# Root of the feed-forward norm moved from GpSimd to VectorE, and new ranks for the instruction order of a two-layer recurrent block

## The chip, the cores and the metric

The kernel is one program on one core of a Trainium2 chip. The metric is device time in microseconds, the median over runs of one launch; lower is better. Times inside the program come from one profiled execution.

## What is computed

Two layers over x of shape (4, 512, 128): batch B = 4, T = 512 tokens, D = 128. Each layer is `x = x + attention(xn) * silu(experts(xn))`, with `xn` the layer norm of `x`.

```python
x = L0_attn_x
xn = _layernorm(x, axis=-1)
s = _L0_attn_ref(xn, ...)              # 16 heads of 8; keys of the last 64 tokens; weighted scores
g = _silu(_L0_ffn_ref(xn, ...))        # 8 experts 128-512-128, gelu, one chosen per token
x = x + s * g
xn = _layernorm(x, axis=-1)
s = _L1_attn_ref(xn, ...)              # norm, windowed attention, projection, residual, and:
#   h = layernorm(out, ln2_g, ln2_b)
#   h = gelu(h @ w1 + b1);  h = h @ w2 + b2;  return h + residual2
g = _silu(_L1_ffn_ref(xn, ...))        # 8 experts 128-512-128, relu, one chosen per token
x = x + s * g
```

The first half of the change is in the `layernorm(out, ln2_g, ln2_b)` of layer 1's own feed forward: the term `1 / sqrt(v + EPS)` for each token.

## The kernel before, in words

**Tiles.** Tokens lie on the 128 partitions. A batch is NT = 4 tiles of 128 tokens; 16 tiles in all. For the experts the tokens of all batches are sorted by expert into NBLK = 23 blocks of 128 rows for each layer.

**Threads.** The work is written as 32 Python generators ("threads"), each a chain of steps over its batches, tiles or blocks. Layer 0: `prepare0` (norm, gate), `route` (sorts tokens to blocks), `moe_load` and `moe_load_2` (a gather of a block's tokens, issued by GpSimd, and its weights), `moe_x`, `moe_h`, `moe_y` (transpose, first and second matrix of a block; `moe_y` ends in a scatter of the block, issued by GpSimd, L666), `gates`, `project0`, `scores_q`, `fitness0`, `masked0` (q spread over heads by GpSimd, L1069), `scores_k`, `values0`, `outs0`, `combine0`. Layer 1: `prepare1` (norm, its root by GpSimd at L442), the same expert threads, `project1`, `queries1` (its q4 is made by GpSimd, L1251), `scores_k1`, `values1`, `outs1`, `contexts1`, `feed1`, `combine1`.

**Order.** Each engine runs its instructions in the order in which it was given them. That order is settled at build time by `run`: a greedy planner that holds a time `now["T"]` for TensorE and a list of taken slots for VectorE ("D"), ScalarE ("A"), GpSimd ("G") and SyncE's queue ("Q"). At each turn it takes, among the threads' next steps, the one that can start first, and among those that can start now the one with the lowest rank. A thread has four ranks, one for each batch (for the expert threads, for each quarter of the blocks). Each step gives its costs by `spent(cost, steps)`: `cost` is TensorE's time, stretched by `pace()`, and `steps` are the pieces of work on the other engines, put into the first free slot. `settle` then makes the order of the slots the order of the instructions on VectorE, ScalarE and GpSimd. So the ranks, the paces and the costs touch no arithmetic, but together they decide the place of nearly every instruction. Where the planner sees TensorE idle, `awake` adds multiplications with ones (bf16, 128x512), whose result is overwritten, to keep it busy.

**The norm of the feed forward.** `feed1` runs eight times, for each batch and each pair of tiles (u = 0, 2). A turn: projection `pr` into PSUM; residual added by VectorE (L1431); moments (L416, L417); the root; `centred` (L428) writes hn; TensorE transposes it (`tr_hn`); ScalarE copies it as hT; then two matrices with gelu between (`f`, `fy`) and the last add (L1468). The root before is `rsqrt`: VectorE adds EPS (L392), GpSimd raises to the power -0.5 (L393), and VectorE's `centred` waits for it:

```python
nc.vector.tensor_scalar_add(dst, src, eps)                                                    # L392
return nc.gpsimd.tensor_tensor(dst, dst, neghalf[:, 0:1].to_broadcast([P, n]), ALU.pow)       # L393
```

`rsqrt_many`, which `project0` already uses for 128 columns, does the same by VectorE alone: four instructions for x and a first guess from the bits, then three Newton steps of three instructions.

GpSimd's line thus holds, in layer 1: roots of `prepare1` (L442), gathers `xb` (L609), scatters `yt` (L666), `q` (L1251), adds `xr` (L1402, L1437) and the roots `rs_d` (L393).

Of the kernel before, what the change touches and what calls it, by code (L numbers as in the profile page):

```python
# [9 lines left out]
F32 = mybir.dt.float32  # L10
# [6 lines left out]
P = 128  # L17
B, T, D = 4, 512, 128
NT = T // P
H, HD = 16, 8  # L20
G, J = 4, 4
# [15 lines left out]
LN_EPS = 1e-5  # L37
# [20 lines left out]
def two_layers(  # L58
# [212 lines left out]
    def after(event):  # L271

        return None, max(0.0, at[event] - max(now["T"], now["-"]))
# [51 lines left out]
            at[e] = t  # L325

    def pace():
        return 1.8 if now["T"] < 70.0 else 1.12

    def behind_steps(e, t):  # L330

# [57 lines left out]
    def rsqrt(dst, src, eps):  # L389

        n = dst.shape[1]
        nc.vector.tensor_scalar_add(dst, src, eps)  # L392
        return nc.gpsimd.tensor_tensor(dst, dst, neghalf[:, 0:1].to_broadcast([P, n]), ALU.pow)  # L393

    def rsqrt_many(dst, src, scale, eps):

        n = dst.shape[1]
        x = small.tile([P, n], F32, tag="rq_x", name=f"rq_x_{dst.tensor.name}", bufs=1)
        nc.vector.tensor_scalar(x, src, scale, eps, ALU.mult, ALU.add)
        y = small.tile([P, n], F32, tag="rq_y", name=f"rq_y_{dst.tensor.name}", bufs=1)  # L400
        nc.vector.tensor_single_scalar(y.bitcast(I32), x.bitcast(I32), 1, ALU.logical_shift_right)
        nc.vector.tensor_scalar(y.bitcast(I32), y.bitcast(I32), -1.0, float(0x5F3759DF), ALU.mult, ALU.add)
        nc.vector.tensor_scalar_mul(x, x, -0.5)
        z = small.tile([P, n], F32, tag="rq_z", name=f"rq_z_{dst.tensor.name}", bufs=1)
        for i in range(3):
            nc.vector.tensor_tensor(z, y, y, ALU.mult)
            nc.vector.tensor_tensor(z, z, x, ALU.mult)
            nc.vector.scalar_tensor_tensor(dst if i == 2 else y, z, 1.5, y, ALU.add, ALU.mult)
# [83 lines left out]
    def route(mask, n):  # L492
# [7 lines left out]
        with tc.high_priority():  # L500
            ps = bank(f"rk_{n}")
            mm(ps[:, 0 : NTOK * E], before_m, mask.rearrange("p i e -> p (i e)"), start=True, stop=True)
            mm(ps[:, NTOK * E : 2 * NTOK * E], ones, mask.rearrange("p i e -> p (i e)"), start=True, stop=True)
            cnt = of([P, E, NTOK], "cnt")
            nc.vector.tensor_copy(cnt, ps[:, NTOK * E : 2 * NTOK * E].rearrange("p (i e) -> p e i", e=E))
            inc = of([P, E, NTOK], "inc")
            nc.vector.tensor_tensor_scan(
                inc.rearrange("p e i -> p (e i)"), go_on.rearrange("p e i -> p (e i)"),
                cnt.rearrange("p e i -> p (e i)"), 0.0, ALU.mult, ALU.add,
            )  # L510
            some = of([P, E, NTOK], "some")
            nc.vector.tensor_tensor(
                some, inc[:, :, NTOK - 1 : NTOK].to_broadcast([P, E, NTOK]),
                tile_at[:, None, :].to_broadcast([P, E, NTOK]), ALU.is_gt,
            )
            nb = of([P, E], "nb")
            nc.vector.tensor_reduce(nb, some, AX.X, ALU.add)
            ends = of([P, E], "ends")
            nc.vector.tensor_tensor_scan(ends, ones[:, 0:E], nb, 0.0, ALU.mult, ALU.add)

            nc.vector.tensor_tensor(inc, inc, cnt, ALU.subtract)
            starts = of([P, E], "starts")
            nc.vector.tensor_tensor(starts, ends, nb, ALU.subtract)
            nc.vector.scalar_tensor_tensor(
                inc, starts[:, :, None].to_broadcast([P, E, NTOK]), float(P), inc, ALU.mult, ALU.add
            )
            at = small.tile([P, NTOK, E], F32, tag="rt_some", name=f"at_{n}", bufs=1)
            nc.vector.tensor_tensor(
                at, ps[:, 0 : NTOK * E].rearrange("p (i e) -> p i e", e=E), inc.rearrange("p e i -> p i e"), ALU.add
            )  # L530
            nc.vector.tensor_tensor(at, at, mask, ALU.mult)
            rowf = of([P, NTOK], "rowf")
            nc.vector.tensor_reduce(rowf, at, AX.X, ALU.add)
            rows_at = of([P, NTOK], "rows_at", I32)
            nc.vector.tensor_copy(rows_at, rowf)

            blk = of([P, NTOK], "blk", I32)
            nc.vector.tensor_single_scalar(blk, rows_at, 7, ALU.logical_shift_right)
            blkf = of([P, NTOK], "blkf")
            nc.vector.tensor_copy(blkf, blk)  # L540
            placef = of([P, NTOK], "placef")
            nc.vector.scalar_tensor_tensor(placef, blkf, -float(P), rowf, ALU.mult, ALU.add)

            tok_blk = of([P, NTOK, 3, NBLK], "tok_blk", BF16)
            in_blk = tok_blk[:, :, 2]
            nc.vector.tensor_tensor(
                in_blk, blkf[:, :, None].to_broadcast([P, NTOK, NBLK]),
                block_at[:, None, :].to_broadcast([P, NTOK, NBLK]), ALU.is_equal,
            )
            nc.vector.tensor_tensor(  # L550
                tok_blk[:, :, 0], in_blk, tile_at[:, :, None].to_broadcast([P, NTOK, NBLK]), ALU.mult
            )
            nc.vector.tensor_scalar_mul(tok_blk[:, :, 1], in_blk, pidx)
            spent(0.35, [("D", 1.0)] * 7, [("rows", n)])
            in_places = []
            for q in range(2):
                in_place = att_p.tile([P, NTOK // 2, P], BF16, tag="osb0", name=f"in_place_{n}_{q}")
                i = q * NTOK // 2
                for u in range(NTOK // 2):
                    nc.vector.tensor_single_scalar(in_place[:, u], place_at, placef[:, i + u : i + u + 1], ALU.is_equal)  # L560
                in_places.append(in_place)
                spent(0, [after(("rows", n)), ("D", 1.2)], [("places", n, q)])

            past = of([1, NBLK, E], "past")
            nc.vector.tensor_tensor(
                past, ends[0:1, None, :].to_broadcast([1, NBLK, E]),
                block_at[0:1, :, None].to_broadcast([1, NBLK, E]), ALU.is_le,
            )
            ofx = of([1, NBLK], "ofx")
            nc.vector.tensor_reduce(ofx, past, AX.X, ALU.add)  # L570
            which = of([1, NBLK], "which", I32)
            nc.vector.tensor_single_scalar(which, ofx, float(E - 1), ALU.min)
            spent(0, [after(("rows", n)), ("D", 0.8)], [("which", n)])
# [839 lines left out]
    def feed1():  # L1413


        for b in range(B):
            for u in range(0, NT, 2):
                two = slice(u, u + 2)
                f = slice(u * P, (u + 2) * P)
# [11 lines left out]
                nc.vector.tensor_tensor(res[:, two], ps, res[:, two], ALU.add)  # L1431
                mv = moments(res[:, two], f"d{b}_{u}")
                rs = small.tile([P, 2], F32, tag="rs", name=f"rs_d{b}_{u}")
                rsqrt(rs, mv[:, :, 1], LN_EPS)
                centred(hn[:, two], res[:, two], mv, rs)
                spent(1.0, [("D", 0.7), ("D", 0.7), ("G", 1.0), ("D", 0.7)], [("pr", b, u)])
                nc.gpsimd.tensor_tensor(  # L1437
                    res[:, two], res[:, two], row("ffn2")[:, None, :].to_broadcast([P, 2, D]), ALU.add
                )
# [31 lines left out]
    def combine1():  # L1471
# [10 lines left out]
    KQ, Q4 = 1, 2  # L1482
    at["x"] = 0.0
    run([
        (moe_h(0, gelu), 0, 59, 111, 16),
        (scores_k1(), 87, 25, 32, 64),
        (project1(), 92, 81, 14, 102),
        (queries1(), 107, 26, 4, 78),
        (combine0(), 19, 20, 21, 22),
        (moe_load(0, xd0, w1_0, C_B1_0), 109, 42, 85, 68),  # L1490
        (moe_load_2(0, w2_0, b2_0), 18, 74, 23, 2),
        (gates(0, yt0), 56, 5, 6, 8),
        (values1(), 66, 112, 86, 55),
        (prepare0(), 31, 65, 95, 50),
        (moe_load(1, xd1, w1_1, C_B1_1), 35, 84, 34, 38),
        (moe_load_2(1, w2_1, b2_1), 101, 118, 37, 44),
        (scores_q(), 70, 36, 104, 94),
        (moe_x(0), 73, 93, 43, 96),
        (contexts1(), 11, 12, 54, 13),
        (project0(), 88, 106, 63, 62),  # L1500
        (moe_y(0, yt0), 117, 82, 90, 41),
        (moe_x(1), 67, 40, 46, 72),
        (gates(1, yt1), 103, 49, 114, 10),
        (values0(), 48, 15, 115, 124),
        (scores_k(), 33, 1, 58, 97),
        (route(mask0, 0), 45, 100, 24, 76),
        (fitness0(), 79, 61, 91, 69),
        (combine1(), 29, 30, 39, 99),
        (route(mask1, 1), 51, 83, 9, 75),
        (moe_y(1, yt1), 121, 71, 113, 127),  # L1510
        (outs0(), 47, 57, 125, 119),
        (masked0(), 7, 52, 53, 17),
        (moe_h(1, relu), 60, 3, 122, 105),
        (prepare1(), 27, 108, 28, 80),
        (outs1(), 120, 110, 116, 89),
        (feed1(), 126, 98, 123, 77),
    ])


# [42 lines left out]
```

## Time and profile before

| what | us |
|---|---|
| median of 3 runs | 510.99 (509.62 to 512.5) |
| time of the profiled execution | 499.03 |
| its span, first to last instruction | 497.3 |
| TensorE busy (multiplications) | 417.26 |
| VectorE busy | 337.45 |
| ScalarE busy | 261.61 |
| GpSimd busy | 179.69 |

The mean granted TensorE clock is 0.918. The span is the sum of what lies between the first and the last instruction; 1.7 us lie around it. In the profile's timeline a row is a start, a length, the engine, the line of the kernel, the operation, output <- input, the shape and the count; in brackets stands the time the engine was idle before and what released it. Table rows for a stretch give busy time and, in brackets, the number of instructions for each engine, then the granted clock, the busy share of the DMA engines and GB/s. A tile's buffer number is left out of its name.

### The profile page before, as it was taken

To read this page: it belongs to the slowest core of one execution; us is meant where nothing else is said; L and a number is where in the kernel's file an instruction comes from. 1 tells how busy PE (TensorE), PEld (TensorE's weight loads), DVE (VectorE), ACT (ScalarE), POOL (GpSimd) and SP (SyncE) were. 2 spreads that over 40 slices of the span, in tenths; PEclk is the share of its full clock that TensorE was granted. 3 is DMA by queue.
4 is the path that set the end of the run, shared out by engine and by line. 5 is a ranking of instruction groups with operands and counts; after the bars stand their busy time and mean duration, and the time that the engine had idled before them with its cause. 6 is when DMAs were issued, how large, how long until landed. Compare 5 with 4: busy or idle time off the path is not lost.

```text
span 497.3 us, 14720 instructions
## 1 busy us (share of the span) xinstructions
PE 417.3 (84%) x5663; PEld 295.0 (59%) x5663; DVE 337.5 (68%) x1013; ACT 261.6 (53%) x513; POOL 179.7 (36%) x251
## 2 busy tenths in 40 slices
PE   5876897998899696599999896878999994699985
PEld 2642565676565462345655574646879883588863
DVE  6899997553846958958774584884677761475565
ACT  1422665697567534375555655444676442246622
POOL 5741455346522222233320304136352335642311
PEclk8787699999999967779999998998999998599999
DMA  5405454756243010100000000051453773352032
GB/s 170 130 1 135 111 156 114 211 152 202 50 109 96 12 54 22 43 22 3 3 22 3 3 1 22 2 150 30 130 140 102 176 200 100 109 134 77 19 105 66
DMA packets 61894, 42.12 MB, mean 85 GB/s; under 512 B 11328, under 2 KB 54208, under 8 KB 61824
## 3 DMA queue, kind: packets, MB, share of 16 engines
q1 hardware_dynamic: 58464, 34.85, 25.3%
q0 software_dynamic: 2944, 6.04, 4.5%
q8 instruction: 45, 0.74, 0.6%
q10 hardware_dynamic: 416, 0.29, 0.3%
q14 instruction: 25, 0.20, 0.1%
HBM read 34.99 MB, written 6.16 MB: 83 GB/s over the span
## 4 chain that ended last, share of the span: by engine, by line
PE 47%; DVE 27%; issue 9%; ACT 7%; POOL 5%; DMA 3%; SPq 0%; POOLq 0%; ACTq 0%; DVEq 0%
PE e L83 8%; PE h L83 6%; PE s L83 5%; PE y L83 4%; PE ov L83 4%; DVE mx L1009 3%; DVE mx L1290 3%; PE fy L83 3%; PE f L83 2%; ACT th L1017 2%; PE o L88 2%; ACT pt L1106 2%; PE qkv L83 1%; PE v L83 1%; DVE sm L1009 1%
## 5 line engine op out<-in xcount | busy, mean ns | idle before, releaser
L666 POOL DMA_INDIRECT yt<-yb,put_at x46 | 46.1, 1002 | 104.3 <-DVE yb L664 24.8
L609 POOL DMA_INDIRECT xb<-xd,tokens_at x46 | 46.2, 1004 | 53.9 <-DVE tokens_at L586 17.1
L83 PE MATMUL y<-wb,hb 128*128 128x128 f32 x368 | 49.7, 285 | 4.3 <-ACT hb L696 3.2
L83 PE MATMUL h<-xbT,wb 128*128 128x128 f32 x368 | 51.2, 291 | 2.3 <-ACT xbT L344 1.3
L83 PEld LDWEIGHTS h<-xbT,wb 128*128 128x128 f32 x368 | 46.5, 202 | 8.5 <-issue 3.3
L83 PEld LDWEIGHTS y<-wb,hb 128*128 128x128 f32 x368 | 46.1, 198 | 7.7 <-ACT hb L696 3.9
L83 PE MATMUL e<-q,kd 32*64 32x256 f32 (+1 forms) x864 | 44.9, 457 | 0.4 <-ACT pt L1106 0.4
L1017 ACT ACTIVATE th<-s 128x768 f32<-128x768 f32 x32 | 26.0, 813 | 29.8 <-DVE mx L1009 29.2
L1333 ACT ACTIVATE pt<-e 128x1024 f32<-128x1024 f32 x32 | 31.0, 1021 | 19.9 <-PE e L83 19.8
L1290 DVE TENSOR_REDUCE mx<-s 128x16 f32<-128x1024 f32 x32 | 37.6, 1218 | 4.4 <-PE s L83 4.2
L83 PE MATMUL s<-k,qd 32*32 32x384 f32 (+1 forms) x1024 | 37.2, 484 | 2.6 <-ACT pt L1333 2.3
L1106 ACT ACTIVATE pt<-e 128x1024 f32<-128x1024 f32 x32 | 31.0, 1021 | 14.2 <-PE e L83 14.1
L83 PEld LDWEIGHTS <-ones 12*64 12x64 bf16 (+2 forms) x439 | 21.5, 107 | 28.6 <-issue 20.4
L1009 DVE TENSOR_REDUCE mx<-s 128x8 f32<-128x768 f32 x32 | 29.3, 949 | 11.9 <-PE s L83 11.9
L344 ACT COPY osb<-ov 128x512 f32<-128x512 f32 x33 | 18.6, 587 | 26.8 <-PE ov L83 21.4
L696 ACT ACTIVATE hb<-h,bb 128x128 f32<-128x128 f32 x92 | 26.5, 382 | 11.3 <-PE h L83 10.2
L1009 DVE TENSOR_REDUCE sm<-th 128x8 f32<-128x768 f32 x32 | 30.0, 946 | 1.3 <-ACT th L1017 1.0
L83 PE MATMUL ov<-pt,va 64*32 64x128 f32 (+1 forms) x896 | 28.8, 290 | 0.4 <-DVE ctx L344 0.2
L83 PEld LDWEIGHTS e<-q,kd 32*64 32x64 f32 x864 | 19.4, 139 | 11.5 <-issue 6.4
L1251 POOL TENSOR_TENSOR q<-qd,jmask 128x640 f32<-128x640 f32 x16 | 20.0, 1260 | 14.7 <-PE e L83 13.4
L83 PE MATMUL e<-sh,ones 12*64 12x256 bf16 (+1 forms) x320 | 20.8, 311 | 3.6 <-DVE sh L1301 3.6
L704 ACT ACTIVATE hb<-h,bb 128x128 f32<-128x128 f32 x56 | 15.8, 376 | 14.7 <-PE h L83 12.0
(287 smaller groups left out, 898.1 us busy)
## 6 DMA issues: line engine op xcount, KB each, us to landing
wb<-in_w SPq DMA_DIRECT2D x92, 256.0 KB
bb<-in_b SPq DMA_DIRECT2D x46, 64.0 KB
acc<-yt SPq DMA_DIRECT2D x8, 256.0 KB
xd<-ln_a SPq DMA_DIRECT2D x4, 256.0 KB
xd<-xr SPq DMA_DIRECT2D x4, 256.0 KB
out<-acc SPq DMA_DIRECT2D x8, 128.0 KB
x<-in_x SPq DMA_DIRECT2D x3, 256.0 KB
bb<-in_cols SPq DMA_DIRECT2D x46, 2.0 KB
```

Of the source, the lines that this page charges most:

```text
L83: ins = nc.tensor.matmul(*args, **kw)
L344: (nc.scalar.copy if e == "A" else nc.vector.tensor_copy)(dst, src)
L609: nc.gpsimd.indirect_dma_start(out=xb, out_offset=None, in_=xd, in_offset=bass.IndirectOffsetOnAxis(ap=tokens_at[:, k : k + 1], axis=0),)
L666: nc.gpsimd.indirect_dma_start(out=yt, out_offset=bass.IndirectOffsetOnAxis(ap=routed[n][0][:, k : k + 1], axis=0), in_=y, in_offset=None,)
L696: nc.scalar.activation(h[:, c, :], src[:, c * P : (c + 1) * P], AF.Gelu, bias=bias[:, c : c + 1])
L704: nc.scalar.activation(dst, src_c, AF.Relu, bias=b)
L1009: nc.vector.tensor_reduce(dst[:, t, 8 * gg : 8 * gg + 8].rearrange("p (u j) -> p u j", u=2), src.rearrange("p u (j f) -> p u j f", j=J), A ...
L1017: nc.scalar.activation(th, ps[gg], AF.Tanh, scale=0.5 * SCALE)
L1106: nc.scalar.activation(pt[:, 2 * gg : 2 * gg + 2], ps[gg], AF.Exp)
L1251: engine.tensor_tensor(dst, src[:, None, o : o + TW].to_broadcast([P, J, TW]), jmask[:, :, None].to_broadcast([P, J, TW]), ALU.mult,)
L1290: nc.vector.tensor_reduce(mx.rearrange("p a g j -> p g a j")[:, 2 * gg : 2 * gg + 2], ps[gg], AX.X, ALU.max, negate=True,)
L1333: nc.scalar.activation(pt[:, 2 * gg : 2 * gg + 2], ps[gg], AF.Exp, scale=SCALE)
```

## The change

Three edits. The root in `feed1` is taken by `rsqrt_many` (13 VectorE instructions on 2 columns, among them the add of EPS) in place of `rsqrt`; its temporary tiles get a common width of 128 columns, of which the first n are used. The planner's costs are altered: the pace of TensorE, the VectorE costs of `route`, and the steps of the norm (four on VectorE in place of two on VectorE, one on GpSimd and one on VectorE). And all 128 ranks are new.

```diff
     def pace():
-        return 1.8 if now["T"] < 70.0 else 1.12
+        return 1.45 if now["T"] < 70.0 else 1.08
...
     def rsqrt_many(dst, src, scale, eps):

         n = dst.shape[1]
-        x = small.tile([P, n], F32, tag="rq_x", name=f"rq_x_{dst.tensor.name}", bufs=1)
+        x = small.tile([P, P], F32, tag="rq_x", name=f"rq_x_{dst.tensor.name}", bufs=1)[:, 0:n]
         nc.vector.tensor_scalar(x, src, scale, eps, ALU.mult, ALU.add)
...
-            spent(0.35, [("D", 1.0)] * 7, [("rows", n)])
+            spent(0.35, [("D", 0.47)] * 7, [("rows", n)])
...
-                spent(0, [after(("rows", n)), ("D", 1.2)], [("places", n, q)])
+                spent(0, [after(("rows", n)), ("D", 0.65)], [("places", n, q)])
...
                 rs = small.tile([P, 2], F32, tag="rs", name=f"rs_d{b}_{u}")
-                rsqrt(rs, mv[:, :, 1], LN_EPS)
+                rsqrt_many(rs, mv[:, :, 1], 1.0, LN_EPS)
                 centred(hn[:, two], res[:, two], mv, rs)
-                spent(1.0, [("D", 0.7), ("D", 0.7), ("G", 1.0), ("D", 0.7)], [("pr", b, u)])
+                spent(1.0, [("D", 0.7), ("D", 0.75), ("D", 0.75), ("D", 0.75)], [("pr", b, u)])
...
     run([
-        (moe_h(0, gelu), 0, 59, 111, 16),
-        (scores_k1(), 87, 25, 32, 64),
-        (project1(), 92, 81, 14, 102),
-        (queries1(), 107, 26, 4, 78),
+        (moe_h(0, gelu), 32, 76, 48, 83),
+        (scores_k1(), 38, 74, 77, 63),
+        (project1(), 115, 64, 19, 52),
+        (queries1(), 61, 28, 17, 69),
...
-        (values1(), 66, 112, 86, 55),
+        (values1(), 86, 20, 30, 112),
...
-        (contexts1(), 11, 12, 54, 13),
+        (contexts1(), 102, 15, 107, 119),
...
-        (moe_y(1, yt1), 121, 71, 113, 127),
+        (moe_y(1, yt1), 85, 11, 114, 53),
...
-        (moe_h(1, relu), 60, 3, 122, 105),
+        (moe_h(1, relu), 120, 99, 66, 95),
...
-        (outs1(), 120, 110, 116, 89),
-        (feed1(), 126, 98, 123, 77),
+        (outs1(), 1, 45, 121, 82),
+        (feed1(), 109, 7, 14, 55),
     ])
```

The called function, with the lines of before:

```python
x = ...                                                                       # [P, n]
nc.vector.tensor_scalar(x, src, scale, eps, ALU.mult, ALU.add)                # L399
nc.vector.tensor_single_scalar(y.bitcast(I32), x.bitcast(I32), 1, ALU.logical_shift_right)
nc.vector.tensor_scalar(y.bitcast(I32), y.bitcast(I32), -1.0, float(0x5F3759DF), ALU.mult, ALU.add)
nc.vector.tensor_scalar_mul(x, x, -0.5)
for i in range(3):
    nc.vector.tensor_tensor(z, y, y, ALU.mult)                                # L406
    nc.vector.tensor_tensor(z, z, x, ALU.mult)
    nc.vector.scalar_tensor_tensor(dst if i == 2 else y, z, 1.5, y, ALU.add, ALU.mult)
```

## The prediction

> **What bounds the kernel now.** I read the page first: the busy row, the slices, the chain by engine.
>
> ```profile
> PE 417.3 (84%) x5663; PEld 295.0 (59%) x5663; DVE 337.5 (68%) x1013; ACT 261.6 (53%) x513; POOL 179.7 (36%) x251
> PE   5876897998899696599999896878999994699985
> PE 47%; DVE 27%; issue 9%; ACT 7%; POOL 5%; DMA 3%; SPq 0%; POOLq 0%; ACTq 0%; DVEq 0%
> ```
>
> TensorE (PE) is the fullest line and nearly half of the chain. VectorE (DVE) carries a quarter, GpSimd (POOL) a twentieth. In the slices (12.4 us each) the digits 4 and 6 after the long run of nines are the hole to look at. The table by stretches measures it:
>
> ```profile
> 345.00:412.00 67.00, 63.89 (x1045) 54.65 (x1045) 45.27 (x133) 39.36 (x94) 25.81 (x29) 1.00 0.55 146
> 412.00:428.00 16.00, 4.24 (x55) 3.25 (x54) 1.43 (x6) 2.29 (x9) 10.67 (x11) 0.72 0.25 67
> 428.00:470.00 42.00, 41.55 (x672) 35.16 (x670) 26.96 (x89) 23.83 (x48) 16.69 (x20) 0.94 0.35 93
> ```
>
> Columns: TensorE, its weight loads, VectorE, ScalarE, GpSimd, then clock, DMA share, GB/s. Before and behind the hole TensorE is full, so time won in it is kept to about 470. In it only GpSimd works. The waits name who held whom, in total us, times, longest:
>
> ```profile
> DVE hn L428 <- POOL rs_d L393: 21.9, 8, 14.6
> PE tr_hn L88 <- DVE hn L428: 13.8, 3, 11.8
> POOL yt L666 <- DMA yt<-yb,put_at: 11.3, 5, 4.2
> ```
>
> So hn waits for the root 21.9 us over eight turns, one wait being 14.6, and TensorE loses 11.8 of that. GpSimd's timeline says why:
>
> ```profile
> 412.49 0.96 POOL L666 DMA_INDIRECT yt<-yb,put_at  x1 [2.09 <-DVE sh L1301]
> 413.76 0.98 POOL L609 DMA_INDIRECT xb<-xd,tokens_at  x1 [0.30 <-PE s L83]
> 417.44 0.96 POOL L666 DMA_INDIRECT yt<-yb,put_at  x1 [2.70 <-ACT hb L704]
> 418.41 2.48 POOL L1251 TENSOR_TENSOR q<-qd,jmask 128x640 f32<-128x640 f32 x2
> 421.06 1.00 POOL L666 DMA_INDIRECT yt<-yb,put_at  x1 [0.17 <-issue]
> ...
> 424.90 1.00 POOL L666 DMA_INDIRECT yt<-yb,put_at  x1 [0.30 <-issue]
> 425.92 0.74 POOL L393 TENSOR_TENSOR rs_d<-rs_d,neghalf 128x2 f32<-128x2 f32 x1
> ```
>
> The root's input was ready at 411.1 (L392 at 410.93), but four scatters, three gathers and two q stood ahead of it. A scatter follows the one before it by 3.6 to 5 us here, since it waits for that one to land. VectorE, held at hn, could release nothing else.
>
> **The root, part by part.** *Removed:* eight powers on GpSimd, 5.9 us busy, off its line, and with them the wait above. *Added:* 13 VectorE instructions a turn for the one at L392, each reading the last one's result. The nearest rows are a chain of the same kind on four columns:
>
> ```profile
> 195.35 0.17 DVE L437 TENSOR_SCALAR w<-mv_b 128x4 f32<-128x4 f32 x1
> 195.56 0.18 DVE L438 RECIPROCAL w<-w 128x4 f32<-128x4 f32 x1
> 195.77 0.16 DVE L439 TENSOR_TENSOR w<-w,mv_b 128x4 f32<-128x4 f32 x1
> ...
> 300.71 0.95 DVE L439 TENSOR_TENSOR w<-w,mv_b 128x4 f32<-128x4 f32 x1
> ```
>
> Start to start is 0.205, so a turn's chain takes 13 x 0.205 = 2.67 us up to hn. Against this stands the Trainium skill, "VectorE: DVE Perf Modes", section "The TRN2 errata": 58 cycles plus the elements at 0.96 GHz, so 60 / 0.96 = 62 ns here and 13 x 62 = 0.8 us, and the change would even shorten the last turn (1.05 now). In this trace small instructions that do not depend on each other do start 0.06 to 0.07 apart (8.55, 8.61, 8.67 us). This chain depends at every link, so I take 205 ns.
>
> Now each turn. From L392's start to hn's the seven unheld turns take 0.99, 0.98, 1.73, 2.02, 1.92, 1.20 and 1.05 us, in sum 9.9; the new ones 7 x 2.67 = 18.7. That is 8.8 us more of VectorE's line. What of it sets the end:
>
> - The last two turns are a bare chain (pr, norm, tr_hn, hT, f, fy). TensorE waits 1.26 and 0.75 us for hn there already:
>
> ```profile
> 485.69 0.17 DVE L392 TENSOR_SCALAR rs_d<-mv_d 128x2 f32<-128x2 f32 x1
> 486.74 0.60 DVE L428 TENSOR_SCALAR hn<-xr,mv_d,rs_d 128x128 f32<-128x128 f32 x2 [0.89 <-POOL rs_d L393]
> ```
>
>   All the excess is paid: 2.67 - 1.20 and 2.67 - 1.05, together 3.1.
> - The turn at 464.8 has 0.4 us of slack before its transpose and pays 0.75 - 0.4, say 0.4.
> - The other four turns (7.0 less their own powers, 5.0 us) are covered by other tiles' work on TensorE: tr_hn comes 2 to 8 us after hn (283.4, 301.0, 345.1, 367.4). Behind them on VectorE queue sh, mx and yb of other threads. At the chain's share of VectorE, 27%, they cost 1.3; bounds 0 and 5.
> - Contention. The row at 300.71 took 0.95 instead of 0.16 while GpSimd ran a q (300.38 to 301.63). The skill, "GPSIMD Engine Reference", section "Key points", says that GpSimd's interfaces to the memory are shared with VectorE, with contention when a VectorE instruction has two inputs there: nine of the thirteen have. Without it the term is nothing; the row gives 0.8 for each chain that meets a q. Twelve q's of 1.25 us, each in reach of a chain for 3.9 us, in the last 232 us, make it a fifth of eight chains: 1.3 us of VectorE, say 0.5 on the path.
>
> Sum of the cost: 3.1 + 0.4 + 1.3 + 0.5 = 5.3.
>
> *The stall returned.* TensorE stopped at 415.43 and resumed at 427.19. Without the power VectorE makes hn by about 415, TensorE goes on at 415.5 with tr_hn, a transpose and y (3.0 us at half clock, 427.2 to 430.2), and next wants e, which needs a q from GpSimd. These come at 419.7 and 420.9, as the scatters ahead of them stay. So e starts near 420 instead of 430.2: 9.3 to 10.5 won. What is late next is q. The clock was 0.50 from 420 to 432 after the idle time, which could add 1 to 2; it may go to VectorE, whose instructions queued up then. I take 10; bounds 8 and 12.
>
> Net with the old order: 5.3 - 10 = -4.7.
>
> **The order.** The ranks move nearly all instructions, on every queue: TensorE, VectorE, ScalarE, GpSimd's gathers and scatters, SyncE's weight loads. No row shows the new order, so I bound it. Gain: TensorE's idle time outside the stall that an order could fill is 9.8 us in 187 to 210, 10.8 in 300 to 345 and 6.9 after 470, in sum 27; a third, 9, is the most I allow, since the new order starts from the same dependences. Loss: one new hole like the old, 10 to 12 us, or two. Are the new costs nearer to the trace? The granted clock was 0.82 in the first 75 us, 1.22 times the full-speed time, so 1.45 is nearer than 1.8. The route's row work took about 4.5 us of VectorE (318.8 to 324.8, less what lay between); 7 x 0.47 with gaps is 4.0, the old 7.7. But eight in_place take 1.35 (0.168 apart), and 0.65 is farther off than 1.2. The norm adds up from rows to 0.46 + 0.4 + 0.34 + 2.67 + 0.6 = 4.5, and the plan gives it 3.25: hn will be over 1 us later than planned, eight times. And the plan still knows nothing of a scatter waiting for the last to land. The better and the worse balance; I take 0 for the order, with -9 and +22 as ends.
>
> So -4.7 of 499.03, the profiled execution's own time (span 497.3 and 1.7 around it): 494.3, or 0.94% less. The median shown is 510.99, 12 above that execution, for which the profile shows no reason; the same share there gives 506.2, and I say 506.0.
>
> **Rivals.** *The new order has its own hole (slower).* Mechanism: q, m4, gathers and scatters still share GpSimd's line, and q is directly what TensorE's e waits for. Place: the stretches with scatters (64 to 195, and 335 to 470), where an attention step's q is put behind several scatters whose y come in a bunch. Price: the distance of three scatters, 412.49 to 421.06, 8.6 us, and 2 for the half clock after it: 10.6. It decides once TensorE waits over 4.7 us in sum, which one bunch does: 510.99 + 10.6 - 4.7 = 517; with two, 527. For it: 20.4 us of q's waits in GpSimd's own list are for e's, so the buffers run tight. Against it: TensorE lost at most a few us by q in the old order.
>
> *The gain is eaten (same).* The longer chain is planned too short, VectorE has 9 us more in a stretch where it is 60 to 70% full, and all of the 5.0 us falls on the path with contention: 5.3 + 3.7 + 1 - 10 = 0: 511. For it: VectorE is 27% of the chain. Against: TensorE is full beside it.
>
> *The order also closes older holes.* -4.7 with the 9 above: 497. For it: the early pace now fits the clock. Against: the worse costs named.
>
> *The change does not do what it says* only if hn still waits as long for its place on VectorE, behind an instruction that itself waits for GpSimd: roots of prepare1 (L442, 1.65 us each, 5.3 waited) stay there. Its time is that of the first two rivals.
>
> **Numbers.** Half a per cent, 2.6 us, is about what a measurement of this kernel can tell from no change: 508.4 to 513.5 is "same". Forecast, 502 to 508.4: 0.32. Older holes closed, below 502: 0.13. Eaten: 0.12. A new hole: 0.43, most of it 514 to 524. So faster 0.45, same 0.12, slower 0.43. For 8 in 10 I leave out below 496 (0.07) and above 524 (0.12). The likeliest case's own range is 502 to 508.4.
>
> **What would show it.** Right: no rs_d on GpSimd; eight chains of 13 on VectorE with starts 0.2 apart; tr_hn's waits under 3 us each; VectorE busy up by 8 x 12 x 0.165 = 16, to about 353; the hole at 412 gone, and the last two turns 1.5 us longer from L1431 to hn. Wrong: a new stretch of over 5 us in which TensorE stands and GpSimd's line shows scatters; tr_hn still waiting over 5 us; starts near 0.07 in the chain; or the expert stage of layer 1 starting (first xb, 331 now) over 5 us later, which would be the order alone.

## The result, and the profile after

The change made the kernel slower: a median of 532.27 us (528.96 to 533.13) against 510.31 (504.39 to 512.5) for the kernel before on the same chip, a ratio of 1.0459 with a 95% interval of 1.0354 to 1.0563. The prediction was 506.0 with a range up to 524, so even the range missed it by 8 us. The profiled execution took 533.13 us, with a span of 531.4.

First the busy row, the slices and the granted clock of the page after, in slices of 13.3 us, then the chain by engine:

```profile
PE 435.4 (82%) x5674; PEld 302.7 (57%) x5674; DVE 346.7 (65%) x1095; ACT 263.0 (50%) x525; POOL 172.9 (33%) x243
...
PE   5963789997998775679979987969898787999875
...
PEclk8786798998999995857979998989998979999988
...
PE 54%; DVE 27%; ACT 8%; issue 6%; DMA 3%; POOL 1%; another core or an unknown queue 1%; SPq 0%; ACTq 0%; DVEq 0%; POOLq 0%
```

The power is gone from GpSimd: its share of the chain fell from 5% to 1% and its count by eight. VectorE has 82 more instructions and 9 us more work. TensorE has nearly the same work (5674 multiplications, 5663 before) and is busy for 18 us longer. Its granted clock fell from 0.918 to 0.900, which makes 8 of the 18 (417.3 x 0.918 / 0.900 = 425.7); the other 10 are not explained. Its idle time, the span less the busy time, rose from 80 to 96. No 6 or 4 stands alone near the end as the hole of before did. Instead the digits 5, 6, 7, 9 ahead of the middle of the row (199 to 252 us) go with a clock of 5, 8, 5, 7.

The waits after (total us, times, longest) that answer to the three shown of before:

```profile
POOL xr L1437 <- DVE hn L428: 43.9, 7, 16.8
...
POOL yt L666 <- DMA yt<-yb,put_at: 11.6, 4, 3.7
...
PE tr_hn L88 <- DVE hn L428: 10.0, 6, 2.9
```

GpSimd now waits for hn, where hn had waited for GpSimd. TensorE's longest wait for hn fell from 11.8 to 2.9 us, in sum from 13.8 only to 10.0. The wait that I set out to predict did go, and the kernel lost 22 us elsewhere.

**Where they went.** Layer 1's tokens are sorted (`tokens_at`, L586, second time) at 330.5 before and at 348.4 after: 18 us are lost there already, with two of the eight feed-forward turns done and no scatter of layer 1 issued. The last output is issued at 494.5 and 528.6, so 16 more follow. These 34 are counted from the profiled execution of before, which was 11 us below its median; between medians the loss is 22. A second profiled execution of before (experiment 5), which lies nearer to the median, has 330.9 and 503.4: 17.5 lost up to the sorting, and 8 behind it. The stretch that makes most of the 18 is the passage from layer 0 to layer 1. The table by stretches, before:

```profile
197.00:222.00 25.00, 19.14 (x233) 10.37 (x232) 17.50 (x44) 12.33 (x24) 7.43 (x8) 0.72 0.11 33
222.00:244.00 22.00, 20.83 (x369) 12.73 (x362) 17.54 (x51) 11.75 (x22) 6.85 (x8) 1.00 0.01 3
244.00:260.00 16.00, 15.43 (x298) 9.85 (x298) 11.43 (x40) 9.36 (x16) 6.18 (x5) 1.00 0.06 19
```

and after:

```profile
197.00:222.00 25.00, 15.33 (x170) 8.88 (x168) 17.27 (x42) 12.24 (x23) 8.20 (x10) 0.71 0.08 23
222.00:244.00 22.00, 16.72 (x195) 7.97 (x179) 14.39 (x29) 5.78 (x9) 0.00 (x0) 0.50 0.00 1
244.00:260.00 16.00, 14.84 (x286) 8.09 (x272) 12.93 (x33) 7.23 (x12) 3.33 (x3) 0.97 0.01 3
```

TensorE's busy time by the granted clock gives its work in full-speed time: 19.14 x 0.72 + 20.83 + 15.43 = 50 us before, and 15.33 x 0.71 + 16.72 x 0.50 + 14.84 x 0.97 = 34 after. So 16 us of work are missing from these 63 us (an estimate, as the two orders do different work there). Half of it is idle time, 16.1 against 7.6; the other half is the clock of 0.50 for 22 us, with 195 multiplications where there were 369. GpSimd does nothing in those 22 us.

There are two places in it where TensorE stands. The first is the largest stop of the whole execution. It is seen in VectorE's timeline after, and what TensorE makes of it:

```profile
198.19 1.21 DVE L956 TENSOR_TENSOR qk<-qk,rsq 128x1024 f32<-128x1024 f32 x1
...
203.11 1.82 DVE L428 TENSOR_SCALAR xr<-x,mv_b,rs 128x128 f32<-128x128 f32 x4 [1.81 <-POOL rs L442]
...
205.12 0.28 DVE L1195 TENSOR_TENSOR projb<-projb,rowb 128x128 f32<-128x128 f32 x1
```

```profile
205.46 1.11 PE L88 MATMUL tr_k<-ident,qk 128*128 128x128 f32 x4 [7.65 <-DVE projb L1195]
```

TensorE's next work, tr_k, had its input qk by 199.40. It was let go by projb, an addition of 0.28 us that reads a bank of PSUM (the memory TensorE writes its results to) filled at 193.82, and which the new order puts on VectorE behind the whole norm of layer 1, and so behind a root on GpSimd, for which VectorE stood 1.81 us. That is the sort of wait the prediction looked for in the root of the feed forward; the new order made it with another root. But this stop does not begin the half clock: from 212 to 220 us the granted clock is 1.00 again, and the kernel before has a stop of 5.39 us in the same passage:

```profile
207.40 1.88 PE L83 MATMUL lg<-gate_sb,xnT 128*128 128x8 f32 x8 [5.39 <-ACT xnT L344]
```

The 0.50 of the 22 us begins at 221, at a second place, a row of shorter stops at the attention scores `s`:

```profile
219.88 0.34 PE L83 MATMUL s<-band_q,diag 32*128 32x384 bf16 x2 [1.57 <-ACT th L1017]
...
224.42 2.87 PE L83 MATMUL s<-k,qd 32*64 32x256 f32 x32 [1.99 <-ACT th L1017]
...
228.61 0.50 PE L83 MATMUL s<-band_q,diag 32*128 32x384 bf16 x2 [1.33 <-DVE mx L1290]
...
234.28 1.35 PE L83 MATMUL e<-bands_k,diag 32*32 32x512 bf16 x16 [1.24 <-ACT th L1017]
```

TensorE stands there for VectorE's maximum (mx) and ScalarE's th of scores that it has just made, and the order has little other work between them. That the stops bring the half clock is argued from their place; no run here removes them alone.

### The profile page after: what moved, and what is told of

Its sections match the earlier page's. It is cut to its first block, busy times and chain, and to the rows that moved or that the text cites. A ratio compares the mean times of both kernels' runs of the same rounds, so it can differ in the third digit from the quotient of the medians.

```text
span 531.4 us, 14818 instructions
## 1 busy us (share of the span) xinstructions
PE 435.4 (82%) x5674; PEld 302.7 (57%) x5674; DVE 346.7 (65%) x1095; ACT 263.0 (50%) x525; POOL 172.9 (33%) x243
## 4 chain that ended last, share of the span: by engine, by line
PE 54%; DVE 27%; ACT 8%; issue 6%; DMA 3%; POOL 1%; another core or an unknown queue 1%; SPq 0%; ACTq 0%; DVEq 0%; POOLq 0%
PE e L83 9%; PE s L83 7%; PE y L83 7%; PE h L83 6%; PE ov L83 5%; DVE mx L1290 4%; PE f L83 3%; PE fy L83 3%; ACT th L1017 3%; PE o L88 2%; DVE mx L1009 2%; PE v L83 1%; DVE xr L428 1%; PE pr L83 1%; PE tr_o L88 1%
## 5 line engine op out<-in xcount | busy, mean ns | idle before, releaser
L609 POOL DMA_INDIRECT xb<-xd,tokens_at x46 | 45.1, 981 | 56.7 <-PE xt L88 18.7
L83 PE MATMUL e<-q,kd 32*64 32x256 f32 (+1 forms) x864 | 46.6, 476 | 0.7 <-issue 0.7
L83 PE MATMUL s<-k,qd 32*64 32x256 f32 (+1 forms) x1024 | 38.7, 491 | 2.9 <-ACT th L1017 2.0
L83 PE MATMUL ov<-pt,va 64*32 64x128 f32 (+1 forms) x896 | 33.4, 294 | 4.2 <-issue 2.8
L696 ACT ACTIVATE hb<-h,bb 128x128 f32<-128x128 f32 x92 | 26.0, 384 | 7.5 <-issue 5.6
L704 ACT ACTIVATE hb<-h,bb 128x128 f32<-128x128 f32 x64 | 17.8, 375 | 17.1 <-PE h L83 9.6
L83 PEld LDWEIGHTS ov<-pt,va 64*32 64x32 f32 (+1 forms) x896 | 18.3, 108 | 13.8 <-issue 7.2
```

Source lines behind the costliest of these rows:

```text
L83: ins = nc.tensor.matmul(*args, **kw)
L609: nc.gpsimd.indirect_dma_start(out=xb, out_offset=None, in_=xd, in_offset=bass.IndirectOffsetOnAxis(ap=tokens_at[:, k : k + 1], axis=0),)
L696: nc.scalar.activation(h[:, c, :], src[:, c * P : (c + 1) * P], AF.Gelu, bias=bias[:, c : c + 1])
L704: nc.scalar.activation(dst, src_c, AF.Relu, bias=b)
```

## The experiments

"Order" here is what ranks and costs decide together. The planner's clock `now["T"]` when the last step is placed I took for its forecast of the kernel; I call it the planner's own end. It is 506.5 for the kernel before and 492.9 for the change. It is TensorE's time alone, which matters from experiment 11 on.

My theory on seeing the result was ORDER: the new order loses time by itself, and the root is near nothing. The rival was ROOT: the chain of 13 on VectorE costs more than worked out. For what makes an order slow, PLAN says that the chip follows the planner's own end, and FIT that ranks only suit the costs and the kernel they were found with, so that any other order comes out late against its plan. RANKS is a form of it in which the new ranks are slow under any costs.

**1. The root alone, in the order of before.** All ranks, costs and slots of before are kept. The twelve links behind the add stand where centred stood:

```diff
-                rsqrt(rs, mv[:, :, 1], LN_EPS)
+                links = rsqrt_links(rs, mv[:, :, 1], 1.0, LN_EPS)   # rsqrt_many as a generator
+                next(links)                                        # the add of EPS, at the old add's place
...                                                                 # GpSimd's slot is held, and left empty
+                for _ in links: pass
                 centred(hn[:, two], res[:, two], mv, rs)
```

> The root by 13 VectorE instructions, with the ranks, costs and slots of before: the first link stands where the add of EPS stood, the other twelve directly ahead of the centring, and GpSimd's slot stays empty. Theory ORDER (the new order alone made the kernel slower, the root is a small gain): 504 to 509 against 510, the wait of hn for GpSimd gone and the hole at 412 with it. Theory ROOT (the longer chain on VectorE is what costs): 520 or more.

Measured: 511.08 against 509.12, ratio 1.0041 (1.0013 to 1.0069). Neither figure was met. The root gains nothing in the old order; it costs 2 us (0.7 to 3.5 by the interval). That is nearer to the cost side of my sum (5.3) alone than to the sum with the stall returned (5.3 - 10).

**2. The order alone, with the old root.** The change with the power back on GpSimd, in the change's plan.

```diff
-                rsqrt_many(rs, mv[:, :, 1], 1.0, LN_EPS)
+                nc.vector.tensor_scalar_add(rs, mv[:, :, 1], LN_EPS)
+                nc.gpsimd.tensor_tensor(rs, rs, neghalf[:, 0:1].to_broadcast([P, 2]), ALU.pow)
```

> The changed kernel with the root given back to GpSimd, ranks, costs and VectorE's slots as in the change. ORDER: 528 to 540, as slow as the change or slower, since hn waits in GpSimd's line again. ROOT: 515 or less.

Measured: 525.63, ratio 1.0268 (1.0179 to 1.0357). The order alone loses most of it, less than the 528 to 540 that I expected of it. The half-clock stretch of the change is there without one Newton step in this place:

```profile
222.00:244.00 22.00, 18.66 (x196) 8.80 (x197) 12.84 (x28) 6.92 (x11) 1.25 (x1) 0.50 0.00 1
```

and TensorE stood 6.72 us before tr_k for projb. By medians the root costs 532.27 - 525.63 = 6.6 in this order, by the two ratios (1.0459 and 1.0268) 10. The two intervals touch, so its size is loose.

**3 and 4. Costs and ranks, each alone, with the new root.** New costs with the ranks of before, and the costs of before with the new ranks. In summary, with the kernel before in the first line:

| kernel | paces, early and late | route's two costs | steps of the norm | ranks |
|---|---|---|---|---|
| before | 1.8, 1.12 | 1.0, 1.2 | with ("G", 1.0) | before |
| 3 | 1.45, 1.08 | 0.47, 0.65 | 0.75 three times | before |
| 4 | 1.8, 1.12 | 1.0, 1.2 | as before, GpSimd's slot empty | new |

> The changed kernel with the 128 ranks of before; paces, route's and norm's costs and the Newton root as in the change. If the new ranks are the bad half (RANKS): 505 to 513. If the new costs are (COSTS: paces too quick for the chip): 525 to 535. If a rank vector is only good with the costs it was found for (FIT): as slow as the change or slower, 530 to 545; the planner's own end is 528 here, where it is 506 for before and 493 for the change.

> Paces and costs of before, the 128 new ranks, the root by VectorE in the held slots. RANKS: 525 to 535. COSTS: 505 to 513. FIT: 525 to 545; the planner's own end is 527 here.

Measured: 560.07, ratio 1.0971 (1.0892 to 1.1049), above all three expectations, and 536.93, ratio 1.0464 (1.036 to 1.0568). The ranks of before are far worse with the new costs than with their own; the new ranks are as slow with the old costs as with their own (1.0464 and 1.0459). The new costs do not make a better order by themselves.

**5. The kernel before, profiled again.** No edit.

> The kernel before, profiled a second time. If the hole at 412 belongs to the order (HOLE): hn waits over 10 us for a root in GpSimd's line again. If it was an accident of the one execution shown (ACCIDENT): no wait of hn over 3 us, and TensorE's idle time lies elsewhere; then the Newton root with the old order had little to win, which the 1.004 measured for it would explain.

Measured: 507.93. The waits of this second execution:

```profile
DVE hn L428 <- POOL rs_d L393: 9.0, 7, 3.2
...
PE tr_hn L88 <- DVE hn L428: 2.0, 2, 1.3
```

The wait of 14.6 us on which the prediction rests is not there, and this execution is 9 us longer than the one that had it. In GpSimd's timeline the root stands behind q and scatters as before:

```profile
422.81 2.47 POOL L1251 TENSOR_TENSOR q<-qd,jmask 128x640 f32<-128x640 f32 x2
...
430.97 0.73 POOL L393 TENSOR_TENSOR rs_d<-rs_d,neghalf 128x2 f32<-128x2 f32 x1
```

The same power came at 425.92 in the first profile, so GpSimd's line is 5 us later here. TensorE was further behind than that: ScalarE had read layer 1's e of the twelfth tile at 395.6 in the first profile and at 406.1 in the second. In the first profile TensorE was 10 us ahead, reached hn early, and gave most of its lead back in the hole: the next e begins at 430.18 in the first profile and at 434.09 in the second. By its last multiplication it is 9 us ahead again; what gave it that is not shown. The execution with the hole is not the slower one.

**6, 7 and 8. One cost at a time**, ranks of before. In 6 the new root with its new planned steps; in 7 the two paces alone; in 8 the two costs of the route alone:

```diff
6  -spent(1.0, [("D", 0.7), ("D", 0.7), ("G", 1.0), ("D", 0.7)], ...)
6  +spent(1.0, [("D", 0.7), ("D", 0.75), ("D", 0.75), ("D", 0.75)], ...)
7  -return 1.8 if now["T"] < 70.0 else 1.12
7  +return 1.45 if now["T"] < 70.0 else 1.08
8  -[("D", 1.0)] * 7 ... ("D", 1.2)
8  +[("D", 0.47)] * 7 ... ("D", 0.65)
```

> Before with the norm's half of the change alone, as written: Newton root and its four steps of cost; ranks, paces and the route's costs as before. Theory PLAN (a rank vector is worth what the planner's own end says with the costs it is used with, and any change of a cost throws the fit away): the planner's end goes from 506 to 519, so 518 to 530 against 509. Theory ROOT-ONLY (only the instructions count): 509 to 513, as with the old order held.

> Before with the two paces of the change alone; ranks, route's costs, root as before. The planner's end is 517 in quicker paces, which is 536 at the old ones (its 20.3 of cost before 70 us by 0.35 and 317 after by 0.04, 19.8 us, are only the paces). PLAN: 532 to 550. If quicker paces do not change what an order is worth (PACE IS SCALE): 505 to 513.

> Before with the route's two VectorE costs of the change alone; ranks, paces, root as before. The planner's end falls from 506 to 501. PLAN: 498 to 509, the one part of the change that helps. If any order other than the one that the ranks were found with is worse (FIT): 515 or more.

Measured: 524.53, ratio 1.0372 (1.0275 to 1.047); 523.53, ratio 1.0296 (1.0228 to 1.0364), between the two theories; and 510.88, ratio 1.0017 (0.9961 to 1.0073), no difference. Kernel 6 does the work of kernel 1 in another order. Altering four numbers that no engine sees cost it 3.3% more, and the plan had it so: its end moved from 506.5 to 519.0. The profile of kernel 8 has a hole of the first profile's kind again, without being slower:

```profile
DVE hn L428 <- POOL rs_d L393: 17.1, 7, 11.4
```

**9 and 10. The paces again.** The early pace alone in the kernel before; and the change with both old paces.

```diff
9   -return 1.8 if now["T"] < 70.0 else 1.12
9   +return 1.45 if now["T"] < 70.0 else 1.12
10  -return 1.45 if now["T"] < 70.0 else 1.08
10  +return 1.8 if now["T"] < 70.0 else 1.12
```

> The kernel before with one number altered: the planner's pace of TensorE in the first 70 us is 1.45 (as in the change) in place of 1.8; root, ranks, late pace and all other costs are those of before. The planner's own end is 506.2 against 506.5, by another order. PLAN (the chip follows the planner's own end plus 3 to 10 us as long as the late pace is the old one): 507 to 516. FIT (the ranks and costs of before are fitted to what the chip did, and any other order is late against its plan): 517 to 530.

> The change with the two paces of before (1.8 and 1.12); its root by VectorE, its ranks, route costs and norm costs stay. The planner's own end is 519.0 against 492.9 with the new paces. PLAN, with the plan's optimism in the paces: 519 plus 3 to 10, so 522 to 529, faster than the change although its plan is 26 us longer. FIT (ranks serve only the very costs that they were found with): 537 or more, slower than the change's 532.

Measured: 513.36, ratio 1.0105 (1.0074 to 1.0137), as PLAN had it; and 537.68, ratio 1.046 (1.0353 to 1.0566), as FIT had it. So the paces are not what spoils the change: with the old ones it is as slow.

**11 and 12. Ranks searched anew.** The planner's own end suggested a version to beat both: the ranks of before, changed a few at a time, a change kept when the planner's own end got no longer. 11 does it with the new root and its planned steps (519.0 became 498.3), 12 with the kernel before as it is (506.5 became 496.0). Paces and route costs are those of before.

```diff
-        (feed1(), 126, 98, 123, 77),
+11      (feed1(), 113, 79, 112, 42),
+12      (feed1(), 122, 105, 36, 27),
...
```

> The root by VectorE and the change's costs for the norm step; paces and route costs of before; and ranks searched anew from those of before until the planner's own end was short: 498.3 against 506.5 in the kernel before and 519.0 with the ranks left (its control is the same search with the root on GpSimd, run beside this one). PLAN (with the late pace of before the chip follows the planner's own end plus 3 to 10 us; the change lost since its shorter plan came from its paces and not from its order): 501 to 508, faster than before. FIT (ranks that win in the plan win there by its errors, and come out later on the chip than single edits of the old plan do): 515 to 530, slower than before.

> The kernel before with its own costs, paces and root by GpSimd; only the ranks are searched anew from those of before until the planner's own end was short: 496.0 against 506.5. PLAN: 499 to 506, faster than before. FIT: 510 to 525, no faster than before although its plan is 10.5 us shorter; and if it stands as far above its plan as the refit with the root by VectorE does, the root has no part in that.

Measured: 518.98, ratio 1.0227 (1.0159 to 1.0296), and 521.08, ratio 1.0268 (1.0211 to 1.0324). Both are slower than before, though the planner's own ends are 8 and 10 us shorter. These are the numbers that FIT gave, but not its reason. The passage from layer 0 to 1 is intact in 11 (19.45 x 0.73 + 20.16 + 15.12 = 49 us of full-speed work in the same three stretches, 50 before). The loss is at the end. TensorE's row in slices of 13 us, in the second profile of before, in 11 and in 12:

```profile
PE   5876887999999667599998987789889888899885
PE   5975987999998956989997979889899968988840
PE   5875889997987687598999897789999899898840
```

and the last of TensorE, of the scatters and of the outputs in 11:

```profile
495.65 1.95 PE L83 MATMUL fy<-fw_sb,f 128*128 128x128 f32 x16
...
497.12 0.98 POOL L666 DMA_INDIRECT yt<-yb,put_at  x1 [2.00 <-DVE yb L664]
...
L1479 SPq DMA_DIRECT2D out<-acc x8: 372/396/460, 505.2 to 515.3; - x8
```

TensorE was done when the plan said so: its last multiplication ends at 497.6 and 499.2, where the planner's own ends are 498.3 and 496.0. But both kernels go on for 20 us behind it, where every other kernel here goes on for 4. The last scatter of layer 1 is issued at 497.1 and 498.2, where the two profiles of before have 469.4 and 477.5, and the loads of its result, the gates, the last products and the outputs come behind it. Those steps take no TensorE time, and `run` does not move `now["T"]` for them, so the search was free to push them back. The plan itself has the tail: its time for the last output (the latest `at["acc", 1, b]`) is 510.7 in the kernel before, 523.8 in 11 and 520.9 in 12. Read by that time, the two searches made the plan longer, and the chip followed it. The root by VectorE has no part in it, as both kernels have the tail.

All orders together, with the planner's own end, the plan's last output and the measured median:

| kernel | ranks | planner's own end | plan's last output | measured | measured less last output |
|---|---|---|---|---|---|
| refit, VectorE's root | searched | 498.3 | 523.8 | 519.0 | -5 |
| before | before | 506.5 | 510.7 | 510.3 | 0 |
| refit, GpSimd's root | searched | 496.0 | 520.9 | 521.1 | 0 |
| norm only | before | 519.0 | 523.2 | 524.5 | 1 |
| early pace only | before | 506.2 | 510.4 | 513.4 | 3 |
| paces only | before | 516.6 | 520.8 | 523.5 | 3 |
| old costs, new ranks | new | 527.3 | 531.5 | 536.9 | 5 |
| route costs only | before | 500.9 | 505.1 | 510.9 | 6 |
| change with old paces | new | 519.0 | 523.2 | 537.7 | 15 |
| new costs, old ranks | before | 527.8 | 532.0 | 560.1 | 28 |
| the change | new | 492.9 | 497.1 | 532.3 | 35 |

Read by the last output, eight of the eleven come within 6 us of the plan, among them the two with searched ranks and one with the new ranks. So PLAN, read this way, holds for these, and an order does not come late only because its ranks are new or were searched. The three that come out 15 to 35 late, the change among them, are the only ones in the table with the new costs of the route and of the norm together; each of the two alone comes within 6. Whether the two together are the cause was not tested with all else held.

## Why the prediction was wrong, step by step

**"The stall returned" (-10) failed first.** The hole was read from one execution as a loss that any other order would keep. The second profile has no such hole and is longer. TensorE's wait in the first was, for the most part, a lead of 10 us given back to a GpSimd line whose scatters I had left where they were. With all else held, moving the root cost 2 us net, where my sum had a gain of 4.7.

**"I take 0 for the order" failed next, and by more.** Measured with the old root: a ratio of 1.0268, some 14 to 17 us, within the end of +22 that I gave and far from the value. The reason given for 0, that the better and the worse new costs balance, does not touch the matter: the ranks of before go with their own costs, and both mixtures measured (3 and 4) were slower than the change or its equal. What stood in place of 0 is, for the larger part, the passage from layer 0 to layer 1, with its stops and the half clock: with the old root, too, the tokens of layer 1 are sorted 16 us later than before (346.5). I also argued costs as if truth made a better order; the route costs, nearer to the trace in part, made no difference, and a truer plan of the norm cost 3.3% (6 against 1).

**The cost of the root, 5.3, was of the right size.** It is 2 in the old order and 7 to 10, loosely, in the new. Its terms: links start 0.19 to 0.20 apart, in the timeline of kernel 1, where L422 to L424 are the three links of a step:

```profile
427.07 0.15 DVE L422 TENSOR_TENSOR rq_z_rs_d<-rq_y_rs_d 128x2 f32<-128x2 f32 x1
427.26 0.16 DVE L423 TENSOR_TENSOR rq_z_rs_d<-rq_z_rs_d,rq_x_rs_d 128x2 f32<-128x2 f32 x1
427.45 0.16 DVE L424 SCALAR_TENSOR_TENSOR rq_y_rs_d<-rq_z_rs_d,rq_y_rs_d 128x2 f32<-128x2 f32 x1
```

So the row of before held against the 62 ns that the prediction worked out from the Trainium skill, "VectorE: DVE Perf Modes", section "The TRN2 errata". That section goes on to say that its 58 cycles are too few for a single instruction and that the measured fixed term is about 150; for 2 columns this makes an estimate of 158 ns, which agrees with the length of the links here, 0.15 to 0.16, though not with their distance. The bare chain of the last two turns took 2.39 and 2.37 us up to hn, where I had 2.67, and 2.5 more than before together instead of 3.1. Contention was too small at 0.5 for all turns. The timeline after, where one turn meets two q:

```profile
439.50 2.46 POOL L1251 TENSOR_TENSOR q<-qd,jmask 128x640 f32<-128x640 f32 x2 [2.74 <-ACT qd L1233]
439.52 1.24 DVE L408 SCALAR_TENSOR_TENSOR rq_y_rs_d<-rq_z_rs_d,rq_y_rs_d 128x2 f32<-128x2 f32 x1
...
440.95 1.03 DVE L406 TENSOR_TENSOR rq_z_rs_d<-rq_y_rs_d 128x2 f32<-128x2 f32 x1
...
443.88 0.50 PE L88 MATMUL tr_hn<-ident,hn 128*128 128x128 f32 x2 [2.90 <-DVE hn L428]
```

Two links of 0.16 took 1.24 and 1.03, 2 us more in all. Other threads' hb stood between the links, and hn came 4.9 us after the chain's start (438.52 to 443.39) in place of 2.67; TensorE's longest wait for hn, 2.90, ends there. So the chain is lengthened by what the planner puts between its links as well, which my sum did not have.

**The rivals.** "The new order has its own hole" had the sign and, short of the 532 measured, the size (517 to 527). At 0.43 it was the likeliest single case, and yet the number was taken from the case with 0.32, which the prediction calls the likeliest. But its mechanism was not what happened; a forecast that rested on it would have had its sign by luck. No stretch of over 5 us had TensorE standing at scatters. The largest stop was 7.65 at tr_k, behind projb on VectorE, and half of the work missing in the 63 us of the passage is clock and not standing.

**What would show it.** No rs_d on GpSimd, starts 0.2 apart, tr_hn's waits under 3 each, the hole gone: all came. The last two turns are 0.6 and 1.3 us longer from L1431 to hn, where 1.5 was expected. VectorE rose to 352.0 in kernel 1, as worked out (353), but only to 346.7 in the change. The one sign that spoke of the order alone, the first xb of layer 1 over 5 us later, came with 18. All signs of the root were right, and they said nothing of the time.

**What stays open.** Why the change and its two relatives in the table come 15 to 35 us behind the plan's last output is not shown. The last 8 to 16 us of the change, behind 348, are spread over the clock and stops of up to 3.5 us.

## What to carry to other kernels

A long wait in one profile is a loss only if the work behind it could have gone on: ask which line sets the pace of the stretch, and profile a second execution before building a sum on one gap. When an edit comes with a new order of all instructions, cost the order first and separately, since here it weighed more than the edit it came with. Before searching on a planner's number, see what it leaves out: TensorE's time alone let two searches add 16 us behind TensorE's end, which the plan's time for the last output would have shown.

## What the runs showed of the hardware

The same program, in the same order, had TensorE's longest wait for hn at 11.8 us in one execution and 1.3 in the next; apart from the first profiled one (499) its 73 runs lay between 504 and 518 us.

A VectorE addition or product that meets GpSimd's q is stretched by far more than the 0.8 us known from before. In kernel 1, on VectorE and GpSimd:

```profile
419.10 3.50 DVE L1267 TENSOR_TENSOR k<-kd,jmask 128x640 f32<-128x640 f32 x1
```

```profile
419.43 2.47 POOL L1267 TENSOR_TENSOR q<-qd,jmask 128x640 f32<-128x640 f32 x2
```

k takes 0.8 alone and 3.50 here: it begins ahead of the two q and ends behind both.

The granted clock stayed at 0.50 from 222 to 244 us after the change. For the last 8 of these TensorE was busy without a break:

```profile
236.00:240.00 4.00, 4.00 (x33) 1.45 (x18) 1.54 (x6) 1.85 (x2) 0.00 (x0) 0.50 0.00 0
240.00:244.00 4.00, 4.00 (x57) 3.06 (x56) 1.91 (x8) 0.09 (x1) 0.00 (x0) 0.50 0.01 4
```

The Trainium skill, "TensorE: Matmul & The Clock Gate", section "Part 1: The HAM clock gate", has the clock go full after about 3.4 us of sustained work; by that rule it would have been full from about 240, and this stretch some 2 us shorter (an estimate). The trace does not agree.
